# Rearranging what the graph stage issues around its matmuls: x loads, raw LSTM weight loads, staged sums, degree operations

## The chip, the cores and the metric

The kernel runs on one core of a Trainium2 chip. The metric is device time of one execution in microseconds (us), as the median of several executions. All data is float32.

## The reference

Four layers are applied to x of shape (128, 64, 256), each as x + layer(relu(layernorm(x))). Only the first one is touched by the change:

```python
h = relu(einsum('ts,bsh->bth', adj, x @ Wg0 + bg0))      # graph convolution 1
h = relu(einsum('ts,bsh->bth', adj, h @ Wg1 + bg1))      # graph convolution 2
for p in range(1, 5):                                    # windows of p tokens
    nw   = 64 // p
    wins = h[:, :nw * p].reshape(128 * nw, p, 256)
    last = lstm_last(Wih[p-1], Whh[p-1], bih[p-1], bhh[p-1], wins)
    h    = h.at[:, arange(nw) * p + (p - 1)].set(last)   # last state of each window
# layer 1: normalised adjacency (A + I scaled by 1/sqrt(degree)) and two batch norms
# layer 2: three products with diagonal, upper and lower part of adj;  layer 3: causal attention
```

The degrees of layer 1, deg = row sums + column sums - diagonal of A + I, are worked out early, beside the graph convolutions, because the engines have room there.

## The kernel before

**Two stages matter here.** The graph stage computes both graph convolutions for all tokens and leaves relu(h) transposed in the tiles hT. The LSTM stage then runs the four LSTMs out of hT. The tokens are cut into 16 slabs (NS = 16) of 512 tokens, four chunks of 128 each. One slab passes through three rounds of the graph stage: layernorm, aggregation with adj and the product with Wg0 in the first, aggregation again in the second, the product with Wg1 in the third. Three slabs are in flight at any time.

**The Strassen-like product.** The product with Wg1 uses seven half-size products instead of eight (`product`, L493). It needs four differences of the activations, which GpSimd makes (`sums`, L485), and matching sums of weights, which are made once (`weight_sum`, L313). The LSTM products do the same, in a form with more sums for p = 2, 3 and 4. Those weight sums are made on GpSimd during the graph stage and kept in DRAM until their LSTM runs. This is the staging:

- For each p of 2, 3, 4 the raw weights come in three groups of DMAs, issued by the SP queue (L363): W1 and W2 (the two halves of Whh, four DMAs of 128 KB each) and R (Wih, eight DMAs). They go to one working buffer, `wbf`, which all three p share, so each group can only be loaded when the sums before have been stored out of that part.
- 28 pieces of GpSimd work follow, each one instruction: additions 256 wide (L313), 512 wide (L370) and 384 wide (L377).
- Seven stores go back to DRAM, on the SP queue (L373, L394). The stores W1 (after piece 17), S4 (after piece 25) and S3 (after piece 27) are those that the next p's loads of W1, W2 and R must wait for.

The LSTM for p = 1 needs no such staging, only the tile `wih` (four loads at L308) and four sums of its own, 512 wide.

**The order is written by hand.** Every step is put into a list `events` with a time in planned microseconds, called order units below. The list is sorted by these times and the instructions are issued in that order. The times are not due times: each engine has its own queue, runs its instructions in the order of the list, and runs ahead as far as its waits allow. A round is `ROUND` = 10 units; slab s starts at 10 s. A staging piece n sits in slot n, six slots to a round:

```python
r, k = divmod(n, 6)
events.append((30 + ROUND * r + (-0.7, 0.5, 1.7, 2.9, 4.1, 5.3)[k], len(events), fn, ()))
```

In units modulo a round, GpSimd's order is: six pieces (-0.7 to 5.3), the four `sums` (7.2 to 8.05), the `root` of a layernorm (8.1, L439). "Round 90" below means the pieces that are placed from 89.3 on and the block of `sums` and root after them.

**VectorE's order** mixes the steps of three slabs: `stats` of the layernorm (L433, L434), then the input of the root (L438), `weighed` (L470, reads PSUM), the second step of the layernorm `shift` (L442, which waits for GpSimd's root and sits 3.0 units after it), and `begun` and `add` (L500, L507), which take the Strassen products out of PSUM. ScalarE copies the aggregated tiles out of PSUM (`aggregated`, L458), and applies the ReLUs (L446, L475, L523). PSUM has eight banks, taken in turn, so TensorE can start a product only when the add that reads the bank's former content has run.

**x loads.** `load` (L424) fetches one slab of 512 KB into one of three `xt` buffers. It is placed 21 units ahead of the slab, while the slab's `stats` start 15.1 units ahead.

**Degrees.** `adjacencies` is a generator with four steps, each run by `next` in one round: lbias, the sums of rows, the diagonal, and a last step with four VectorE instructions (L179 to L182). Then `degrees_root` (GpSimd, L185), `degrees` (VectorE, L189) and `normalize` (two matmuls at L209 and one VectorE instruction, L210).

Of the kernel before, what the change touches and what calls it, by code (L numbers as in the profile page):

```python
# [20 lines left out]
def kernel(ctx: ExitStack, tc: tile.TileContext, a: dict, out: bass.AP):  # L21
# [11 lines left out]
    NS = NT // SUP  # L33
# [132 lines left out]
    def adjacencies():  # L166

        nc.vector.tensor_add(lbias, con["bih"], con["bhh"])
        yield


        scr = first.tile([P, P], F32, tag="scr", name="scr")
        nc.vector.tensor_add(scr, adj_bd, ident)
        nc.vector.reduce_sum(deg[:, 0:1], scr, axis=AX.X)
        yield
        nc.vector.tensor_mul(scr, scr, ident)
        nc.vector.reduce_sum(deg[:, 1:2], scr, axis=AX.X)
        yield
        nc.vector.tensor_add(ahT, adjT_bd, ident)  # L179
        nc.vector.reduce_sum(deg[:, 2:3], ahT, axis=AX.X)  # L180
        nc.vector.tensor_add(deg[:, 0:1], deg[:, 0:1], deg[:, 2:3])
        nc.vector.tensor_sub(deg[:, 0:1], deg[:, 0:1], deg[:, 1:2])  # L182

# [3 lines left out]
    def degrees():  # L187
        dd = first.tile([P, P], F32, tag="dd", name="dd")
        nc.vector.tensor_scalar_mul(dd, ident, deg[:, 3:4])  # L189

        return dd
# [15 lines left out]
    def normalize(dd):  # L207
        ps = bank()
        nc.tensor.matmul(ps[:, :P], ones, dd, start=True, stop=True)  # L209
        nc.vector.scalar_tensor_tensor(ahT, ahT, deg[:, 3:4], ps[:, :P], op0=ALU.mult, op1=ALU.mult)  # L210
# [92 lines left out]
    def load_lstm(src, tag, pool):  # L303
        w = pool.tile([P, 7, 4, P], F32, tag=tag, name=tag)
        v = src.rearrange("(c p) (g h m) -> h c p g m", p=P, g=4, m=P)
        for h in range(2):
            for c in range(2):
                nc.sync.dma_start(w[:, 2 * h + c], v[h, c])  # L308
        return w

    def weight_sum(w, k):
        op = nc.gpsimd.tensor_sub if k else nc.gpsimd.tensor_add
        op(*(w[:, m] for m in ((S1, A21, A22), (S2, S1, A11), (S3, A11, A21), (S4, A12, S2))[k]))  # L313
# [96 lines left out]
    ROUND, HALF = 10.0, SUP // 2  # L410
    with tc.tile_pool(name="pa", bufs=2) as pa, tc.tile_pool(name="pax", bufs=3) as pax:
        events, wih0, made = [], [], []

        def graph_part(s):
            t0, v = ROUND * s, {}

            def at(t, fn, *args):
                events.append((t0 + t, len(events), fn, args))
# [104 lines left out]
                nc.scalar.activation(graphs(s, o), v["h2"][:, o, :].rearrange("p (q d t) -> p q d t", d=2, t=T),  # L523
                                     AF.Relu)

            at(-21, load)
            if s == 0:
                at(-20.5, first_constants)
                at(-10.5, second_constants)
# [16 lines left out]
            late, end = 0, s == NS - 1  # L546
# [8 lines left out]
            for c in range(KC):  # L555
                t = (0.86, 2.6)[c] if end else 4.35 + 0.89 * c
# [17 lines left out]
            at(late + 4.0, add, 0, 1, "b")  # L574
            at(late + 4.4, add, 1, 1, "a")
            at(late + 5.0, relu2, 0)
            at(late + 6.6, begun, 1, 0, "a")
            at(late + 7.1, relu2, 1)

            if s == 0:  # L580
# [5 lines left out]
                at(-9.5, lambda: weight_sums(con["wg1"]))  # L586
            if s == 4:
                pieces = adjacencies()
                for k in range(4):
                    at(5.0 + ROUND * k, next, pieces, None)  # L590
                at(11.5 + ROUND * 3, degrees_root)
                at(13.3 + ROUND * 3, lambda: made.append(degrees()))
            if s == 5:
                at(0, lambda: wih0.append(load_lstm(a["WihT"][0], "wih", lwa)))
            if s == 9:
                at(5.0, lambda: normalize(made[0]))
            if s == 9:
                for k in range(4):
                    at(1.4 + 1.3 * k, lambda k=k: weight_sum(wih0[0], k))

        for s in range(NS):
            graph_part(s)

        def stage(n, fn):
            r, k = divmod(n, 6)
            events.append((30 + ROUND * r + (-0.7, 0.5, 1.7, 2.9, 4.1, 5.3)[k], len(events), fn, ()))

        for i, p in enumerate(range(2, NL + 1)):
            work, stores, loads = staging(p)
            for n, fn in enumerate(work):  # L610
                stage(28 * i + n, fn)
            for n, fn in stores.items():
                stage(28 * i + n + 1, fn)
            for n, fn, t in zip((18, 26, 28), loads, (10.5, 17.5, 24.5)):
                if i:
                    stage(28 * (i - 1) + n + 1, fn)
                else:
                    events.append((t, len(events), fn, ()))
        for _, _, fn, args in sorted(events, key=lambda e: e[:2]):
            fn(*args)  # L620
    graph_weights.close()
# [105 lines left out]
    events = []  # L727

    def at(t, fn, *args):
        events.append((t, len(events), fn, args))  # L730
# [154 lines left out]
    def first_step(t0, st, tags, names):  # L885

        p, N = st["p"], st["N"]
        input_ = input_sums(st, 0)
        for k in (-9, -8.5, 0.2, 0.4) if st["new"] else (*((-0.8, -0.6) if p == NL else (-3.4, -1.4)), 2.6, 6.6):
            at(t0 + k, next, input_)  # L890
        g, end, t = {}, {}, t0
        for (name, gi, fn), tag in zip((g for g in GATES if g[0] != "f"), tags):
            g[name], end[name] = gate(t, st, p - 1, gi, fn, tag, names)
            t += 7
        e = end["g"]
        cell = cells[st["s"]]

        def start(n):
            i, g_ = (gates[g[k]["tag"]][:, n, :, :N] for k in "ig")
            nc.gpsimd.tensor_mul(cell[:, n, :, :N], i, g_)  # L900

        def squash(n):
            nc.scalar.activation(gates[g["g"]["tag"]][:, n, :, :N], cell[:, n, :, :N], AF.Tanh)

        h_at = t + 13.3
        for n in range(2):
            at(e + 2.2 + 0.1 * n, start, n)
            at(e + (6.07, 9)[n], squash, n)
            at(h_at + 0.8 * n, state, st, n, g["o"], g["g"], p == 1)
        st["h_at"] = h_at + 0.8  # L910
        return t
# [202 lines left out]
    t, tags = 0.0, [0, 1, 2, 3, 4]  # L1114
    plan(t, 2, (2, load_r), *((8 + 3 * k, fetch, name) for k, name in enumerate(("X", "W1", "W2", "S1", "S2"))),
         (25, fetch, "S4", 2, 7), (28, fetch_s3, 0))
    for p in range(1, NL + 1):
        pairs = pairs_of(p)
        for k in range(0, len(pairs), 2):
# [3 lines left out]
            for i, st in enumerate(sts):  # L1123
                if p == 1:
                    t = first_step(t, st, [tags[(3 * (k + i) + n) % 5] for n in range(3)], FIRST_BANKS)
                else:
# [4 lines left out]
                    t = first_step(t, st, tags[:3] if i == 0 else [*tags[3:], tags[0]], GROUP_BANKS)  # L1131
# [9 lines left out]
            for j in range(1, p):  # L1141
                for st in sts:
                    fin = p == NL and j == p - 1 and st is sts[-1]
                    u = t
                    t = outer_step(t, st, j, now, fin)
# [104 lines left out]
    with tc.tile_pool(name="pz", bufs=1, reuse_waits="tile") as pz:  # L1250
# [14 lines left out]
        events = []  # L1265
# [220 lines left out]
        late = ctx.enter_context(tc.tile_pool(name="late", bufs=1, side="right", reuse_waits="tile"))  # L1486
# [55 lines left out]
    with tc.tile_pool(name="pc", bufs=2, reuse_waits="tile") as pc, \  # L1542
            tc.tile_pool(name="pc1", bufs=1, reuse_waits="tile") as pc1:
        events = []
# [403 lines left out]
```

## Time and profile before

| what | us |
|---|---|
| median of 3 runs | 1836.33 (1835.55 to 1836.90) |
| the profiled execution, own time | 1838.82 |
| its span | 1837.10 |
| TensorE busy in the span | 1802.4 |
| graph stage, from the start to the first LSTM matmul | 178.70 |

The span is what the profile shows of the execution, from its first to its last instruction; the execution's own time also holds what lies around that (1.72 us here). The profiled execution is 2.49 us above the median of the runs. PE is TensorE's matmuls, PEld its weight loads, DVE VectorE, ACT ScalarE, POOL GpSimd and SP the queue that issues nearly all DMAs. In the timelines a line gives start, duration, engine, line of the kernel, operation, output and inputs, the number of like instructions that are merged, and in brackets how long the engine had been idle and what ended that. The granted TensorE clock was 1.00 in every stretch of the graph stage that is shown.

### The profile page before, as it was taken

Reading aid. Unit: us, or ns where it says so; the run is one execution under the profiler, and the core shown is the slowest. Engines: PE = TensorE matmul, PEld = TensorE weight load, DVE = VectorE, ACT = ScalarE, POOL = GpSimd, SP = SyncE. Lnnn points to the kernel's source line nnn. Section 1 sums busy time; section 2 is a strip of 40 time slices with the busy share of each in tenths; the row PEclk is TensorE's granted clock in tenths of the full one; section 3 lists DMA queues with packets and bytes.
Section 4 is the critical chain, followed back from the end, with each engine's and each line's share of the span. In section 5 each row is a group of like instructions: output and inputs, shape, how many; then the busy total and the mean of one; then the engine's idle time right before and its main releaser. Section 6 shows DMA issues by size and latency. Waiting matters only on the chain.

```text
span 1837.1 us, 24418 instructions
## 1 busy us (share of the span) xinstructions
PE 1802.4 (98%) x8532; PEld 1299.3 (71%) x8532; DVE 1196.0 (65%) x2346; ACT 990.8 (54%) x1776; POOL 1211.8 (66%) x1207
## 2 busy tenths in 40 slices
PE   8999999999999999999999999899999999999998
PEld 7987444466566887787466666566444899999997
DVE  6775555565666666666566666778776566666664
ACT  6765666644545545544644444678684444444442
POOL 5898455765766777776677776767354666666663
PEclk9999999999999999999999999999999999999999
DMA  5754300000003000003000000333200110111111
GB/s 149 242 181 174 115 1 0 6 1 9 6 23 115 1 1 1 1 1 113 26 0 1 1 1 30 109 115 115 70 3 1 47 33 26 47 47 47 47 47 35
DMA packets 67498, 91.20 MB, mean 50 GB/s; under 512 B 4784, under 2 KB 57776, under 8 KB 67376
## 3 DMA queue, kind: packets, MB, share of 16 engines
q1 hardware_dynamic: 66928, 89.35, 14.7%
q8 instruction: 68, 1.11, 0.3%
q14 instruction: 54, 0.44, 0.1%
q10 hardware_dynamic: 448, 0.30, 0.1%
HBM read 56.08 MB, written 33.55 MB: 49 GB/s over the span
## 4 chain that ended last, share of the span: by engine, by line
PE 89%; POOL 5%; ACT 2%; issue 2%; DVE 1%; DMA 1%; SPq 0%; POOLq 0%; DVEq 0%; ACTq 0%
PE ps L961 20%; PE ps L985 16%; PE ps L853 14%; PE ps L1672 8%; PE ps L1282 5%; PE ps L1399 4%; PE ps L1759 3%; PE ps L1639 3%; PE ps L454 2%; PE ps L1735 2%; PE ps L464 2%; PE ps L493 2%; PE ps L1769 2%; PE ps L1800 1%; PE ps L700 1%
## 5 line engine op out<-in xcount | busy, mean ns | idle before, releaser
L972 DVE TENSOR_TENSOR gate<-gate,ps 128x512 f32<-128x512 f32 (+2 forms) x360 | 216.7, 603 | 171.9 <-PE ps L961 160.1
L1005 ACT ACTIVATE gate<-gate,lbias 128x512 f32<-128x512 f32 (+2 forms) x288 | 175.7, 653 | 166.9 <-DVE gate L972 84.2
L866 DVE TENSOR_TENSOR gate<-gate,ps 128x512 f32<-128x512 f32 (+2 forms) x162 | 100.7, 640 | 128.7 <-PE ps L853 118.7
L970 ACT COPY gate<-ps 128x512 f32<-128x512 f32 (+2 forms) x144 | 74.9, 520 | 158.8 <-PE ps L961 158.3
L853 PE MATMUL ps<-tx,wih 128*128 128x512 f32 (+2 forms) x276 | 117.9, 544 | 3.0 <-ACT gate L869 2.5
L1615 ACT ACTIVATE h<-x,ln_rn 128x256 f32<-128x256 f32 x128 | 68.0, 592 | 92.8 <-POOL ln_rn L1612 92.7
L1015 POOL TENSOR_TENSOR gate<-gate 128x1024 f32<-128x1024 f32 (+3 forms) x37 | 73.5, 1986 | 63.1 <-ACT gate L1005 63.1
L862 ACT ACTIVATE gate<-gate,lbias 128x512 f32<-128x512 f32 (+2 forms) x108 | 95.7, 886 | 29.0 <-DVE gate L866 28.9
L1672 PE MATMUL ps<-wl,ag 128*128 128x128 f32 x900 | 108.4, 276 | 0.6
L1672 PEld LDWEIGHTS ps<-wl,ag 128*128 128x128 f32 x900 | 104.2, 192 | 3.3 <-ACT ag L1644 2.5
L961 PEld LDWEIGHTS ps<-h,wb 128*128 128x128 f32 x392 | 70.9, 190 | 41.2 <-issue 21.5
L999 DVE TENSOR_TENSOR gate<-gate,ps 128x512 f32<-128x512 f32 (+2 forms) x144 | 80.7, 602 | 21.6 <-PE ps L985 19.6
L961 PE MATMUL ps<-h,wb 128*128 128x256 f32 (+2 forms) x392 | 91.5, 356 | 1.9 <-POOL wb L947 1.3
L853 PEld LDWEIGHTS ps<-tx,wih 128*128 128x128 f32 x276 | 51.5, 190 | 57.1 <-issue 39.7
L818 POOL TENSOR_TENSOR tx<-hT 128x512 f32<-128x512 f32 (+2 forms) x29 | 36.0, 1242 | 79.2 <-PE ps L853 72.6
L869 ACT COPY gate<-ps 128x512 f32<-128x512 f32 (+2 forms) x108 | 59.4, 550 | 52.4 <-PE ps L853 51.8
L1018 POOL TENSOR_TENSOR cell<-cell,gate 128x1024 f32<-128x1024 f32 (+2 forms) x36 | 73.1, 2030 | 19.9 <-ACT gate L1005 19.9
L985 PE MATMUL ps<-hT,wb 128*128 128x512 f32 x160 | 81.7, 592 | 0.0
L900 POOL TENSOR_TENSOR cell<-gate 128x1024 f32<-128x1024 f32 (+2 forms) x36 | 78.1, 2191 | 5.4 <-ACT gate L862 5.4
L985 PE MATMUL ps<-wih,thA 128*128 128x512 f32 (+2 forms) x192 | 79.3, 495 | 0.0
L853 PE MATMUL ps<-hT,wih 128*128 128x512 f32 (+2 forms) x168 | 78.4, 571 | 0.0
L1021 POOL TENSOR_TENSOR cell<-cell,gate 128x1024 f32<-128x1024 f32 (+3 forms) x37 | 75.5, 2041 | 2.9
(333 smaller groups left out, 4981.5 us busy)
## 6 DMA issues: line engine op xcount, KB each, us to landing
xt<-in_x_dram SPq DMA_DIRECT2D x30, 512.0 KB, 4.4
x1d<-xt SPq DMA_DIRECT2D x16, 512.0 KB, 2.9
x<-x1d SPq DMA_DIRECT2D x16, 512.0 KB, 5.0
out_dram<-x SPq DMA_DIRECT2D x15, 512.0 KB, 3.4
W<-wb SPq DMA_DIRECT2D x6, 896.0 KB, 4.1
wb<-W SPq DMA_DIRECT2D x6, 896.0 KB, 4.9
wb<-in_WihT_dram SPq DMA_DIRECT2D x32, 128.0 KB, 3.4
wb<-in_WhhT_dram SPq DMA_DIRECT2D x24, 128.0 KB, 2.8
```

The lines of the kernel that those rows point to most:

```text
L853: nc.tensor.matmul(wide(p_[:, :N]), wih_of(p, k, gi), x_, start=first_, stop=True, skip_group_check=True)
L862: nc.scalar.activation(to, r[bank_][:, :N] if bank_ else to, fn, bias=lbias[:, l, m : m + 1])
L866: nc.vector.tensor_add(slot(n, hc), slot(n, hc), r[bank_][:, :N])
L900: nc.gpsimd.tensor_mul(cell[:, n, :, :N], i, g_)
L961: nc.tensor.matmul(B[pr, name][:, g * H : (g + 1) * H], w[:, g, :], d, start=(new and g == 0), stop=(name, k) in (("a", 4), ("b", 3), ("c" ...
L972: nc.vector.tensor_add(to, to, v)
L985: nc.tensor.matmul(to, w, d, start=(pr == 1 and c == 0), stop=(c == 1), skip_group_check=True)
L999: nc.vector.tensor_add(part(m, k), part(m, k), v)
L1005: nc.scalar.activation(v, v, FN[r, g], bias=lbias[:, l, b : b + 1])
L1021: nc.gpsimd.tensor_add(cell(n)[:, c], cell(n)[:, c], gate_(("11", "12")[n], 0)[:, c])
L1282: nc.tensor.matmul(r[name], con["w1"][:, OF[j], g, :], x_, start=new, stop=(name, j) in (("a", 4), ("b", 3), ("c", 2)), skip_group_check=True)
L1672: nc.tensor.matmul(v["g", name][:, p_, :], x_[:, m, ts(p_, P)], wl2[:, OF[j], m, :], start=new and p_ == m == 0, stop=m == 2 and (name, j) ...
```

## The change

No instruction that computes is added or removed, and no DMA either. What changes is the place of instructions in the list, and so their order on each engine:

- The x loads of slabs 3 to 15 are placed 26 units ahead of the slab instead of 21.
- The staging starts at slot 3 of a list of slots that begins at 20 instead of 30: three slots into a round one earlier, 6.4 units ahead. After the 28 pieces of p = 2 come the four `wih` sums as pieces of their own (before, they stood at 91.4 to 95.3, besides the six pieces of that round). After the 28 of p = 3 two slots stay empty. The last piece so moves from 165.3 to 171.7.
- The raw loads of a next p no longer stand in the slot after the store that they wait for, but at the end (9.01) of the round in which that slot lies. For p = 3 they stand at 59.01, 69.02 and 79.03 (before: 60.5, 72.9, 75.3), for p = 4 at 109.01, 129.02 and 129.03 (before: 105.3, 120.5, 122.9). Slab 10's x load, for example, moves from behind the R loads of p = 3 to ahead of them. For p = 2 the three are at 9.01, 11 and 19.01 instead of 10.5, 17.5 and 24.5.
- The last step of `adjacencies` is cut in two, so that it takes five rounds. `degrees_root`, `degrees` and `normalize` follow one round later.
- For slab 14 the last `begun` stands at 6.15 instead of 6.6, which puts it ahead of the direct product of slab 15 on VectorE.

```diff
@@ adjacencies
         nc.vector.tensor_add(ahT, adjT_bd, ident)
         nc.vector.reduce_sum(deg[:, 2:3], ahT, axis=AX.X)
+        yield
         nc.vector.tensor_add(deg[:, 0:1], deg[:, 0:1], deg[:, 2:3])
         nc.vector.tensor_sub(deg[:, 0:1], deg[:, 0:1], deg[:, 1:2])
@@ graph_part
-            at(-21, load)
+            at(-21 if s < 3 else -26, load)
...
-            at(late + 6.6, begun, 1, 0, "a")
+            at(late + (6.15 if s == NS - 2 else 6.6), begun, 1, 0, "a")
...
             if s == 4:
                 pieces = adjacencies()
-                for k in range(4):
+                for k in range(5):
                     at(5.0 + ROUND * k, next, pieces, None)
-                at(11.5 + ROUND * 3, degrees_root)
-                at(13.3 + ROUND * 3, lambda: made.append(degrees()))
+                at(11.5 + ROUND * 4, degrees_root)
+                at(13.3 + ROUND * 4, lambda: made.append(degrees()))
             if s == 5:
                 at(0, lambda: wih0.append(load_lstm(a["WihT"][0], "wih", lwa)))
-            if s == 9:
+            if s == 10:
                 at(5.0, lambda: normalize(made[0]))
-            if s == 9:
-                for k in range(4):
-                    at(1.4 + 1.3 * k, lambda k=k: weight_sum(wih0[0], k))
@@ after the slabs
+        START = (9.01, 11, 19.01)
+        PHASE = (-0.7, 0.5, 1.7, 2.9, 4.1, 5.3)
+
         def stage(n, fn):
             r, k = divmod(n, 6)
-            events.append((30 + ROUND * r + (-0.7, 0.5, 1.7, 2.9, 4.1, 5.3)[k], len(events), fn, ()))
-
+            events.append((20 + ROUND * r + PHASE[k], len(events), fn, ()))
+
+        at_piece = 3
         for i, p in enumerate(range(2, NL + 1)):
             work, stores, loads = staging(p)
             for n, fn in enumerate(work):
-                stage(28 * i + n, fn)
+                stage(at_piece + n, fn)
             for n, fn in stores.items():
-                stage(28 * i + n + 1, fn)
-            for n, fn, t in zip((18, 26, 28), loads, (10.5, 17.5, 24.5)):
-                if i:
-                    stage(28 * (i - 1) + n + 1, fn)
-                else:
-                    events.append((t, len(events), fn, ()))
+                stage(at_piece + n + 1, fn)
+            for fn, t in zip(loads, START if i == 0 else after):
+                events.append((t, len(events), fn, ()))
+            full = [at_piece + n for n in (17, 25, 27)]
+            after = [20 + ROUND * ((n + 1 - (n + 1) % 6) // 6) + 9.01 + 0.01 * k for k, n in enumerate(full)]
+            at_piece += 28
+            if i == 0:
+                for k in range(4):
+                    stage(at_piece + k, lambda k=k: weight_sum(wih0[0], k))
+                at_piece += 4
+            else:
+                at_piece += 2
```

## The prediction

> **What bounds the kernel now.** First the page: which engine fills the span, and where the fill is missing.
>
> ```profile
> PE 1802.4 (98%) x8532; PEld 1299.3 (71%) x8532; DVE 1196.0 (65%) x2346; ACT 990.8 (54%) x1776; POOL 1211.8 (66%) x1207
> ...
> PE   8999999999999999999999999899999999999998
> ...
> POOL 5898455765766777776677776767354666666663
> ```
>
> TensorE is busy for 98%, so only its holes can be won. The edit touches the graph stage, the first 182 us (slices 1 to 4). There the list of waits gives TensorE three: "PE ps L493 <- DVE h L507", 2.3 us once, and "<- DVE h L500", 2.8 us twice. I cut the stage from one start of the L464 matmuls (one a round) to the next:
>
> ```profile
> 79.55:89.44 9.89, 9.89 (x64) 9.12 (x63) 7.21 (x20) 7.19 (x13) 6.60 (x10) 1.00 0.77 217
> 89.44:102.25 12.81, 10.51 (x65) 9.41 (x64) 8.46 (x24) 7.57 (x13) 12.20 (x13) 1.00 0.38 142
> 102.25:114.78 12.53, 10.60 (x63) 9.19 (x62) 7.53 (x19) 7.21 (x13) 12.37 (x15) 1.00 0.49 167
> 114.78:124.90 10.12, 10.12 (x63) 9.24 (x62) 7.33 (x18) 7.32 (x13) 9.89 (x13) 1.00 0.73 248
> 124.90:134.95 10.05, 10.05 (x63) 9.28 (x62) 7.38 (x21) 7.38 (x13) 8.56 (x11) 1.00 0.56 188
> 134.95:146.23 11.28, 10.34 (x64) 9.27 (x63) 7.17 (x19) 7.30 (x13) 8.78 (x11) 1.00 0.75 218
> ```
>
> Columns: stretch, length, then busy us of PE, PEld, DVE, ACT, POOL. An undisturbed round takes 10.05 us and is all TensorE; three take 12.81, 12.53 and 11.28. Why, the timelines of DVE, POOL and the DMA queue SP say:
>
> ```profile
> 92.03 0.43 DVE L433 BATCH_NORM_STATS2 ln_st<-xt 128x6 f32<-128x256 f32 x1 [4.19 <-DMA xt<-in_x_dram]
> 110.45 0.68 DVE L442 SCALAR_TENSOR_TENSOR ln_rn<-ln_mv,ln_rn 128x4 f32<-128x4 f32 x1 [2.94 <-POOL ln_rn L439]
> 141.89 0.68 DVE L442 SCALAR_TENSOR_TENSOR ln_rn<-ln_mv,ln_rn 128x4 f32<-128x4 f32 x1 [1.68 <-POOL ln_rn L439]
> ...
> 89.86 2.54 POOL L370 TENSOR_TENSOR wc<-wb 128x512 f32<-128x512 f32 x2 [2.79 <-DMA wb<-in_WihT_dram]
> 98.84 1.27 POOL L313 TENSOR_TENSOR wih<-wih 128x512 f32<-128x512 f32 x1
> 137.29 0.73 POOL L313 TENSOR_TENSOR wb<-wb 128x256 f32<-128x256 f32 x1 [3.47 <-issue]
> ...
> 81.93 5.92 SPq L363 DMA_DIRECT2D wb<-in_WihT_dram  x8
> 87.96 0.96 SPq L424 DMA_DIRECT2D xt<-in_x_dram  x2
> 132.94 1.91 SPq L363 DMA_DIRECT2D wb<-in_WhhT_dram  x4
> ```
>
> **Hole 1** (2.30 us at 97.55): the x load of slab 10 stood behind eight raw-weight DMAs (87.96), VectorE waited 4.19 us for it, and the h2 adds that free PSUM banks stood behind that. **Hole 2** (1.86 us at 111.57): GpSimd had four `wih` sums of 1.24 us besides its six pieces between 96.36 and 106.54; its root came 2.94 us late to VectorE's shift. **Hole 3** (0.94 us at 143.02): GpSimd waited 3.47 us for a raw load which the SP queue could issue only at 132.94, because the S4 store, issued at 125.10, took 7.82 us to land.
>
> **What the Trainium skill says.** "PSUM — Partial Sum Buffer", section "Engine vs sequencer instructions": ScalarE, VectorE and GpSimdE queues are strict FIFO. The trace agrees: at 110.45 VectorE held back ready adds. "DMA: Bandwidth & Descriptors", section "Anatomy of one DMA — SWDGE (gpsimd) path": DMA engines do not wait on semaphores; the issuing sequencer does, before dispatch. Agrees: raw loads (L363) held SP for 12.1 us in four waits on stores. "SBUF — State Buffer", section "Who interferes with whom": a VectorE tensor_tensor with both inputs in SBUF contends with GpSimd's reads. Agrees as far as it goes: the 128x128 add at L179 took 0.72 us, the same form at L173 0.26.
>
> **The ceiling.** Round starts run 29.06, 39.11, 49.16, 59.29, 69.34, 79.39, 89.44, 102.25, 114.78, 124.90, 134.95, 146.23, 156.56, 166.61. From 29.06 to 166.61 are 137.55 us for 13 rounds; 13 x 10.05 = 130.65. Excess 6.90, of which 0.22 is the two matmuls of `normalize`, which only change rounds. So **6.68 us** can come back: the three holes (5.10) and slowed products beside them (two of four at 107.46 wait for `t`, 0.33; first products after a hole and the round after each, 1.25 together).
>
> **Part by part.**
>
> *x loads of slabs 3 to 15, five units earlier in the order.* No DMA is added. On SP, slab 10's load now stands before the eight R loads of p=3 instead of behind. Ahead of it is the S3 store, which waits for GpSimd's last piece of p=2. I place that piece at 74.75: root 8 ends at 73.49, piece 27 takes 1.25. So the load goes out near 75.4, and by the page's median of 4.4 us it lands near 80; VectorE wants it near 87.9. 8 us spare, hole 1 goes. Its xt buffer (three of them) was freed by ReLUs of slab 7, eleven order units earlier, so SP does not stop there. Each earlier load adds 0.4 us of SP time ahead of raw loads. That costs nothing while they have the spare time given below. Slab 3's load now precedes the `parts_d` store, which held SP 4.5 us until 15.07.
>
> *`wih` sums as four pieces between p=2 and p=3, and the staging one round earlier.* GpSimd's work per round is 3.9 us of `sums` and root plus pieces. In an undisturbed round the root ends at 83.64 and the second sum can start at 90.5 (80.45 + 10.05, ScalarE's copy), less 0.7 for the first sum: room for 6.1 us of pieces. With 0.70 us for 256 wide, 1.0 for 384, 1.25 for 512, rounds of pieces before, from 30 on: 4.2, 6.4, 5.3, 5.4, 5.3, 5.85, **10.2**, 5.9, 4.8, 5.3, 6.4, 4.7, 5.9, 5.3. Trace for the bold one: 10.18. After, from 20 on: 2.1, 5.9, 4.75, 6.15, 5.05, **6.9**, 4.75, 6.4, 5.6, 5.1, 3.9, 4.75, 5.85, 5.6, 5.1, tail 3.2. Worst is 6.9, 0.8 over the room. The root has slack: normally it ends 0.96 us before the shift (83.64 to 84.60), and a shift late by 2.94 and 1.68 cost 1.86 and 0.94, so another 0.74 to 1.08 is absorbed. Together 1.7 to 2.0 us; 0.8 fits and the next round (4.75) pays it back. Hole 2 goes. If the cover were gone, 0.8 us.
>
> *Raw loads at fixed places after their stores.* p=3: R's use comes after five 256-wide pieces, at 83.64 + 3.5 = 87.1. W2 needs the S4 store (67.2, lands near 71.2), R's last four the S3 store (74.75, near 78.5); eight issues end by 81, landing 83.5. Spare 3.6 us; the 2.79 wait goes. p=4: S4 is done at 124.5, S3 at 127.0. The S4 store lands after 3.8 us (median of these stores) or 7.8 (longest), W2's loads are out by 130.2 or 134.2 and land by 133 or 137; wanted at 135.2. R, right behind, lands by 136 or 140; wanted at 137.3 at the earliest. GpSimd's wait is 0 to 2.7 us in a round with 1.3 us room and 1.7 slack: TensorE loses **0**. Behind these loads no x load is queued any more. Hole 3 goes. I take 0 and keep 1 us for the range.
>
> *Two empty slots before p=4; later end.* GpSimd's last piece ends at 171.2 by this count (before: 175.1), though later in the order. Its next work, `tx` (L818), waited 6.63 us for hT; with the stage 6.7 us shorter that leaves 2.8. Nothing.
>
> *Degree operations.* The same DVE instructions (0.72 + 0.29, then 0.38 + 0.16) now in two rounds, root (0.55 POOL) and `normalize` a round later; ahT is used only after the LSTM stage. Nothing in a DVE with over 2 us idle a round; with that cover gone 0.5.
>
> *`begun` of slab 14 ahead of the direct product.* 0.47 us of DVE moves from 179.57 to before 178.91. ScalarE's ReLUs run in the old order and start at 179.69 on the direct product, so nothing; bounds -0.4 to +0.3.
>
> *Earlier GpSimd pieces in round 20*: they fill a 4.63 us idle stretch before 28.59. If they slow DVE's small operations, 0 to 0.3.
>
> **Sum.** -6.68, plus 0.3 for DVE contention and rounds that do not close fully: -6.4. Against the profiled execution's own 1838.82 (span 1837.10): 1832.4. That execution lies 2.5 above the median of the runs, so against 1836.33: **1829.9**. What follows is TensorE work in the LSTM stage and shifts as a whole.
>
> **Rivals.** *One hole stays or a new one opens* (R2), for instance in round 70, or after late p=4 loads: 1.5 to 4 us, giving 1831.5 to 1834. For it: POOL is booked with 5.85 us or more in five rounds of 6.1. *No gain* (R3): SP stops before the x loads, since all stores in front of them wait for GpSimd; holes 1 and 3 return elsewhere, 1834 to 1837. Against it: every x load has 8 us or more. *Slower* (R4): the p=4 raw loads, bound to 129 in the order, land so late that GpSimd stands in the middle of round 130 with `sums` 12 behind. TensorE loses the wait less 3.0 us (1.3 + 1.7). It eats the gain from a wait of 9.7 us on, and makes the kernel 0.2% slower from 13.4 on, that is W2 landing at 148.6: some 1840.5. Against it: with the longest store seen W2 lands at 137. That the change does not do what it says is part of R3: order is not time, and SP runs ahead wherever it may.
>
> **Numbers.** A measurement of this kernel can tell about 0.2% (3.7 us) from no change. All holes closed: 0.76, 1829 to 1831. R2 0.13, half of it beyond 1832.7. R3 0.05, R4 0.06. Faster by over 0.2%: 0.76 + 0.06 = 0.82, less 0.03 for holes of which I see only the first layer: 0.79. Within: 0.14. Slower: 0.07. The range reaches from 1828.9 (the end effect of 0.4 and a little below) to 1833.0, into R2.
>
> **What would show it.** Right: round starts 10.0 to 10.1 us apart from 29 to about 160, one 0.22 longer; no L433 wait on xt near 88; no L442 wait over 2 us on L439; `wih` sums near 75; hT's last ReLU some 6.5 us earlier. Wrong: a round over 11 us, a GpSimd wait over 4 us on a raw load, or a first LSTM matmul (178.70 before) later than 175 us.

## The result, and the profile after

| | before, us | after, us |
|---|---|---|
| median of 15 runs each, first comparison | 1837.56 | 1833.29 |
| ratio, first comparison | | 0.9974 [0.9966, 0.9981] |
| ratio, second comparison (`after_again`) | | 0.9977 [0.9967, 0.9987] |
| profiled executions, own time | 1838.82, 1838.52, 1837.41 | 1832.69, 1832.86 |

Faster by 0.26% (4.8 us by the first ratio), where 0.35% (6.4 us) was forecast; 6.4 us lies just outside the first interval, whose faster end is 6.2 us. The first comparison's median includes three disturbed executions (2697, 4866 and 6743 us), which its ratio leaves out, and the profiled execution that came with it, one of them, ran at a granted clock of 0.655, so the trace after is that of `after_again`, the same kernel run again.

The stretches from one round start to the next, in `after_again` (columns as in the prediction: stretch, length, busy us of PE, PEld, DVE, ACT, POOL, then clock and DMA):

```profile
79.01:89.06 10.05, 10.05 (x64) 9.28 (x63) 7.80 (x19) 7.28 (x13) 9.74 (x14) 1.00 0.69 205
89.06:99.11 10.05, 10.05 (x64) 9.28 (x63) 8.89 (x23) 7.35 (x13) 9.49 (x12) 1.00 0.07 26
99.11:109.38 10.27, 10.27 (x66) 9.50 (x65) 7.88 (x22) 7.57 (x13) 8.11 (x10) 1.00 0.83 273
109.38:119.87 10.49, 10.33 (x63) 9.26 (x62) 7.48 (x19) 7.21 (x13) 10.25 (x14) 1.00 0.58 209
119.87:129.92 10.05, 10.05 (x63) 9.27 (x62) 7.45 (x19) 7.38 (x13) 8.44 (x11) 1.00 0.68 230
129.92:139.97 10.05, 10.05 (x64) 9.28 (x62) 7.47 (x19) 7.27 (x13) 8.69 (x12) 1.00 0.82 218
```

The rounds of 12.81, 12.53 and 11.28 us are gone. One round is 0.22 longer for the two matmuls of `normalize`, one 0.44 for a new small loss. The timelines of the same run show what answers to the three waits. VectorE:

```profile
104.28 0.75 DVE L443 SCALAR_TENSOR_TENSOR ln_rn<-ln_mv,ln_rn 128x4 f32<-128x4 f32 x1
```

GpSimd:

```profile
74.31 5.15 POOL L314 TENSOR_TENSOR wih<-wih 128x512 f32<-128x512 f32 x4
87.75 1.30 POOL L371 TENSOR_TENSOR wc<-wb 128x512 f32<-128x512 f32 x1
107.10 2.50 POOL L371 TENSOR_TENSOR wb<-wb 128x512 f32<-128x512 f32 x2 [2.09 <-DMA W<-wb]
138.09 1.31 POOL L371 TENSOR_TENSOR wc<-wb 128x512 f32<-128x512 f32 x1 [0.21 <-issue]
```

The queue SP:

```profile
67.06 0.34 SPq L374 DMA_DIRECT2D S<-wb  x1
76.53 0.38 SPq L425 DMA_DIRECT2D xt<-in_x_dram  x1
76.97 5.46 SPq L364 DMA_DIRECT2D wb<-in_WihT_dram  x8
128.64 2.64 SPq L364 DMA_DIRECT2D wb<-in_WhhT_dram  x4
```

(After the change lines 180 and later stand one line further down, so L443 is the shift.) The shift that had waited 2.94 us no longer waits; the `wih` sums run near 75; the first use of p=3's R at 87.75 does not wait, that of p=4 waits 0.21 us. What is new is the 2.09 us wait of GpSimd at 107.10 for a store. It makes the next root late: the next slab's shift waits 0.62 us for it at 115.26, and TensorE then stands for a moment:

```profile
116.66 0.70 PE L494 MATMUL ps<-g,wg 128*128 128x256 f32 x2 [0.16 <-DVE h L501]
```

The end of the stage, on TensorE:

```profile
172.88 1.98 PE L861 MATMUL ps<-hT,wih 128*128 128x512 f32 x4 [0.55 <-DVE h L501]
174.70 1.02 PE L861 MATMUL ps<-ready,wih 128*128 128x512 f32 x2
175.94 1.13 PE L861 MATMUL ps<-ready,wih 128*128 128x512 f32 x2 [0.22 <-ACT gate L877]
176.91 1.88 PE L861 MATMUL ps<-hT,wih 128*128 128x512 f32 x4
```

In the kernel before, the group that corresponds to the last of these lines was

```profile
183.07 1.88 PE L853 MATMUL ps<-hT,wih 128*128 128x512 f32 x4
```

I use this fourth group of LSTM matmuls as the mark for the end of the stage. It starts at 176.91 (before: 183.07), 16.85 us after the last round start; before it was 16.46.

### The profile page after: what moved, and what is told of

It reads as the page before. It is cut to its first block, busy times and chain, and to the rows that moved or that the text cites. A ratio compares the mean times of both kernels' runs of the same rounds, so it can differ in the third digit from the quotient of the medians.

```text
span 2695.0 us, 24421 instructions
## 1 busy us (share of the span) xinstructions
PE 2680.4 (99%) x8532; PEld 1605.8 (60%) x8532; DVE 1198.1 (44%) x2346; ACT 1006.6 (37%) x1776; POOL 1178.5 (44%) x1207
## 4 chain that ended last, share of the span: by engine, by line
PE 99%; DVE 0%; ACT 0%; DMA 0%; issue 0%; DVEq 0%
PE ps L969 21%; PE ps L993 18%; PE ps L861 17%; PE ps L1680 8%; PE ps L1290 5%; PE ps L1407 5%; PE ps L455 3%; PE ps L465 3%; PE ps L1767 3%; PE ps L1743 3%; PE ps L494 3%; PE ps L1647 2%; PE ps L1777 2%; PE ps L708 2%; PE ps L1808 2%; PE ps L666 1%
## 5 line engine op out<-in xcount | busy, mean ns | idle before, releaser
L861 PE MATMUL ps<-tx,wih 128*128 128x512 f32 (+2 forms) x276 | 172.6, 760 | 0.0
L1680 PE MATMUL ps<-wl,ag 128*128 128x128 f32 x900 | 155.8, 348 | 0.0
L1680 PEld LDWEIGHTS ps<-wl,ag 128*128 128x128 f32 x900 | 150.3, 256 | 4.6 <-ACT ag L1652 2.6
L969 PE MATMUL ps<-h,wb 128*128 128x256 f32 (+2 forms) x392 | 131.9, 475 | 0.7 <-ACT h L670 0.7
L969 PEld LDWEIGHTS ps<-h,wb 128*128 128x128 f32 x392 | 82.1, 211 | 84.4 <-issue 52.3
L993 PE MATMUL ps<-hT,wb 128*128 128x512 f32 x160 | 119.5, 839 | 0.0
L861 PE MATMUL ps<-hT,wih 128*128 128x512 f32 (+2 forms) x168 | 115.4, 806 | 0.0
L993 PE MATMUL ps<-wih,thA 128*128 128x512 f32 (+2 forms) x192 | 114.4, 688 | 0.0
L861 PE MATMUL ps<-tx,wb 128*128 128x512 f32 x144 | 101.4, 838 | 0.0
L969 PEld LDWEIGHTS ps<-tx,wb 128*128 128x128 f32 x288 | 60.8, 215 | 58.5 <-issue 39.0
```

The lines of the kernel that those rows point to most:

```text
L861: nc.tensor.matmul(wide(p_[:, :N]), wih_of(p, k, gi), x_, start=first_, stop=True, skip_group_check=True)
L969: nc.tensor.matmul(B[pr, name][:, g * H : (g + 1) * H], w[:, g, :], d, start=(new and g == 0), stop=(name, k) in (("a", 4), ("b", 3), ("c" ...
L993: nc.tensor.matmul(to, w, d, start=(pr == 1 and c == 0), stop=(c == 1), skip_group_check=True)
L1680: nc.tensor.matmul(v["g", name][:, p_, :], x_[:, m, ts(p_, P)], wl2[:, OF[j], m, :], start=new and p_ == m == 0, stop=m == 2 and (name, j) ...
```

## The experiments

All trace numbers are of one profiled execution each. "13 rounds" is from the third round start (near 29) to the last (near 160 or 166), 137.55 us in the execution on which the prediction was made.

### The changed kernel again, and parts of it

> The changed kernel once more, for its trace at full TensorE clock. My theory (all three holes of 6.68 us in the round starts close): round starts 10.05 us apart from 29 to about 160, total 137.55 - 6.7 = 130.9 for the 13 rounds, ratio 0.9965. The rival, that a hole of 1 to 2 us stays in round 70 or after the late raw loads of p=4: one or two rounds of 11 us or more, 132 to 133 in all, ratio 0.9973.

Measured: 13 rounds in 131.29 us, no round over 10.49. The holes are shut; the ratio, 0.9977, is nearer the rival's.

**x loads alone** (on the kernel before):

```diff
-            at(-21, load)
+            at(-21 if s < 3 else -26, load)
```

> The kernel before with the x loads of slabs 3 to 15 five units earlier and nothing else. If the holes are independent, hole 1 closes and 2.8 us come back (ratio 0.9985). My theory now: between 90.4 and 110 us GpSimd is the chain (its sums at 92.4, root at 95.3, six pieces and four wih sums to 106.5), and an earlier x does not move it; hole 1 shrinks to about 1 us, hole 2 grows by what hole 1 lost, and nothing or under 0.7 us comes back (ratio 0.9996 to 1.0).

Measured: 136.90 us, ratio 1.0003 [0.9994, 1.0011]: nothing. The two rounds together take 26.20 us, and took 25.34. VectorE no longer waits for x near 88, but GpSimd's root comes late, since the first use of R waits longer than before (3.81 us, against 2.79, 3.12 and 1.83 in three traces of the kernel before: the x load now runs ahead of R). The timeline of VectorE in `x_only`:

```profile
97.66 1.22 DVE L442 SCALAR_TENSOR_TENSOR ln_rn<-ln_mv,ln_rn 128x4 f32<-128x4 f32 x1 [2.62 <-POOL ln_rn L439]
111.64 0.68 DVE L442 SCALAR_TENSOR_TENSOR ln_rn<-ln_mv,ln_rn 128x4 f32<-128x4 f32 x1 [3.62 <-POOL ln_rn L439]
```

Of GpSimd and of TensorE:

```profile
91.23 2.56 POOL L370 TENSOR_TENSOR wc<-wb 128x512 f32<-128x512 f32 x2 [3.81 <-DMA wb<-in_WihT_dram]
```

```profile
99.33 0.70 PE L493 MATMUL ps<-g,wg 128*128 128x256 f32 x2 [2.40 <-DVE h L500]
112.77 0.70 PE L493 MATMUL ps<-g,wg 128*128 128x256 f32 x2 [1.86 <-DVE h L500]
```

Hole 1 has another releaser and the same size. GpSimd was the second layer behind the x load; I had not followed it when I gave hole 1 to the x load. My new theory underrated it too (1 us expected, 2.40 measured).

**Staging, raw loads and `wih` sums alone** (the change with the x loads, the degrees and the last `begun` as before):

> The changed kernel with the x loads back at 21 units ahead, and the degrees and the last begun of slab 14 as before: only the staging, the wih sums and the raw loads stand in their new places. In this list slab 10's x load stands at 79.00, just ahead of the R loads of p=3 at 79.03, so theory A says hole 1 closes without the earlier x loads and the whole gain is here: 13 rounds in 130.7 to 131.2 us, ratio as after_again within 0.0003. Rival B, that the x loads need the five units more: a DVE wait of 2 us or more on an x load and 1 to 3 us less gained.

Measured: 130.91 us, no wait on x, ratio 0.9970 [0.9959, 0.9982]. Theory A holds: the whole gain is here. The fourth LSTM group starts 16.46 us after the last round start, as in the kernel before. (Slab 10's x load still goes out just ahead of the R loads here, at 75.57; `raw_slots` below takes that away.)

**Degrees and the last `begun` alone:**

> The kernel before with only the degree operations spread over five rounds and the last begun of slab 14 moved ahead. Theory: no change, 13 rounds in 137.3 to 137.8 us, ratio 0.9997 to 1.0003. Rival: the VectorE block of 1.55 us at 78.3 delays something that hole 1 hides, then up to 0.5 us comes back.

Measured: 136.90 us, ratio 1.0010 [1.0002, 1.0018]. Against my expectation the time is slightly over the kernel before's. The trace shows one new wait: `degrees` on VectorE waits 1.91 us for GpSimd's `degrees_root`, which now stands in the crowded round 90 behind the `wih` sums. TensorE does not stop for it: from 98.36 to 111 it works without a hole, though at half its clock from 99.01 to 102.42 (the clock is taken up in the last section). The 13 rounds lie within those of three traces of the kernel before. The record of the single executions says more: 6 of the 13 of `rest_only` have a mean granted clock of 0.997, against 4 of the 57 of the kernel before, while at 0.999 and 0.998 the two kernels' means lie within 0.5 us of each other. So much of the 0.1% goes with a lower clock; why this kernel has it more often stays open. The stage's end takes 16.45 us.

### The kernel before twice more, the crowded round, the raw loads' places

> The kernel before, unchanged, for a second trace. Theory: hole 3 (1.5 us with the round after it) was the luck of one execution, in which the S4 store of p=3 took 7.82 us; two relatives with the same raw loads had no hole there. Then this trace shows rounds of 10.0 to 10.3 us after 125 and 13 rounds in 136.2 to 137.0 us. Rival: hole 3 belongs to the kernel, a round over 10.8 us between 125 and 160.

> The kernel before, unchanged, for a third trace. As the second: no round over 10.8 us after 125 by the theory that hole 3 is an accident of one store's landing; one such round by the rival. Holes 1 and 2 (rounds of 12 to 14 us between 89 and 116) in both theories.

Measured: 137.67 and 136.16 us. Neither has a round over 10.14 us after 117: hole 3 is the accident of one execution, in which the S4 store took 7.8 us to land (6.2 and 5.8 in these). But my total for `before_b`, at most 137.0, was wrong: these two have something else. One round takes 14.7 us in each, and its mean granted clock is 0.88. Stretches of `before_b`:

```profile
89.12:101.58 12.46, 10.52 (x66) 9.42 (x65) 8.88 (x24) 7.56 (x13) 11.61 (x12) 1.00 0.32 117
101.58:116.26 14.68, 12.49 (x63) 10.86 (x62) 7.36 (x19) 8.12 (x14) 14.45 (x18) 0.88 0.55 194
```

Of `before_c`:

```profile
89.39:104.06 14.67, 12.17 (x66) 10.82 (x65) 8.01 (x24) 7.66 (x13) 13.38 (x15) 0.88 0.43 147
104.06:114.91 10.85, 10.33 (x63) 9.26 (x62) 7.19 (x19) 7.20 (x13) 10.69 (x14) 1.00 0.42 148
```

Just after a hole TensorE runs slowly for some 3.4 us; in `before_b`, on its timeline:

```profile
111.42 0.70 PE L493 MATMUL ps<-g,wg 128*128 128x256 f32 x2 [1.86 <-DVE h L500]
111.96 0.62 PE L493 MATMUL ps<-t,wg 128*128 128x256 f32 x2
112.41 3.45 PE L454 MATMUL ps<-adjT_bd,h 128*128 128x128 f32 x16
```

Sixteen such matmuls take 1.95 us elsewhere. The drop costs 1.5 us here, and 0.17 on the next group (0.77 instead of 0.60).

**The `wih` sums back in round 90** (on the changed kernel):

```diff
-                    stage(at_piece + k, lambda k=k: weight_sum(wih0[0], k))
+                    events.append((91.4 + 1.3 * k, len(events), lambda k=k: weight_sum(wih0[0], k), ()))
```

> The changed kernel with the four wih sums back at 91.4 to 95.3, besides six pieces; their slots in the staging stay empty. Theory: GpSimd's round 90 grows from 6.4 to 11.4 us, root 11 ends near 108.6 instead of 103.6, VectorE's shift (wanted near 104.3) comes 4.3 us late, 0.74 to 1.08 of it is absorbed: a hole of 3.2 to 3.6 us and up to 0.5 us beside it; the 2.09 us wait for the W2 store near 107 goes. 13 rounds in 134.2 to 135.0 us, ratio to the kernel before near 0.9990. Rival: the staging's earlier start alone made the room, and the loss is under 1.5 us.

Measured: 134.44 us, 3.15 more than the changed kernel, inside the range; the median is 1836.87 us, 3.9 over the changed kernel's 1832.98 of the second comparison, and the ratio 0.9999 [0.9990, 1.0008] holds the expected 0.9990 only at its edge. The wait for the W2 store is gone, as said. The loss sits in two places, though, not in one (the timelines of VectorE and of TensorE):

```profile
97.47 1.29 DVE L190 TENSOR_SCALAR dd<-ident,deg 128x128 f32<-128x128 f32 x1 [1.66 <-POOL deg L186]
108.41 0.68 DVE L443 SCALAR_TENSOR_TENSOR ln_rn<-ln_mv,ln_rn 128x4 f32<-128x4 f32 x1 [3.09 <-POOL ln_rn L440]
```

```profile
99.56 0.67 PE L494 MATMUL ps<-t,wg 128*128 128x256 f32 x2 [0.73 <-DVE h L508]
109.54 0.70 PE L494 MATMUL ps<-g,wg 128*128 128x256 f32 x2 [1.86 <-DVE h L501]
```

The degree root stands in the crowded round as in `rest_only` and holds VectorE; the shift then waits 3.09 us and TensorE stands 1.86 us. So the spread of the `wih` sums is worth some 3 us in the trace. The staging's earlier start without it would be worth 2.7 us by traces (134.44 against a mean of 137.13 before), but the ratio allows 1.8 us at most. The profiled execution is one of the quicker ones: six executions with a mean granted clock of 0.999, it among them, took 1835.2 to 1836.8 us, the six with a lower clock 1836.9 to 1839.8.

**The raw loads in the slot after their stores** (on the changed kernel):

```diff
-            full = [at_piece + n for n in (17, 25, 27)]
-            after = [20 + ROUND * ((n + 1 - (n + 1) % 6) // 6) + 9.01 + 0.01 * k for k, n in enumerate(full)]
+            after = [20 + ROUND * ((at_piece + n) // 6) + PHASE[(at_piece + n) % 6] for n in (19, 27, 29)]
```

> The changed kernel with the raw loads of p=3 and p=4 in the slot after the store that they wait for, as in the kernel before; slab 10's x load is then behind p=3's R loads again. Theory: since the whole staging stands 6.4 units earlier, R is out by 83 us and the x load lands by 88, when VectorE wants it; no hole, 13 rounds within 0.5 us of the changed kernel's 131.3. Rival: the order on SP is what made hole 1, then VectorE waits 2 us or more on xt near 88 and a round takes over 11 us.

Measured: 131.54 us. Slab 10's x load goes out at 81.93 behind R's eight, and no DVE wait follows. p=4's R makes GpSimd wait 2.26 us, within the bound of 2.7, and one round takes 10.23: two tenths. The queue SP in `raw_slots`, then the S4 store of p=2 in the kernel before:

```profile
81.93 0.95 SPq L425 DMA_DIRECT2D xt<-in_x_dram  x2
```

```profile
74.91 0.34 SPq L373 DMA_DIRECT2D S<-wb  x1
```

The fixed places bring next to nothing; what shut hole 1 is the earlier start, by which that store goes out at 67.06 (67.08 in `raw_slots`) instead of 74.91.

### The two small losses

**x loads back at 21 units** (on the changed kernel):

> The changed kernel with the x loads of all slabs back at 21 units ahead. Theory: hole 1 stays shut, since the staging's earlier start did that; and slab 12's x load goes out behind the W2 store of p=3 instead of just ahead of it, so that store lands within 6.5 us (8.5 in the changed kernel), GpSimd does not wait 2.1 us for it at 107, and the round of 10.49 us becomes 10.05: 13 rounds in 130.8 to 130.95 us. Rival: the 8.5 us are chance, the wait stays or comes and goes with no tie to the x load, 131.2 to 131.6; or the earlier x loads are needed and a round takes over 11 us.

Measured: 130.86 us; no wait for the W2 store, which landed in 6.1 us. Stretches:

```profile
99.64:109.91 10.27, 10.27 (x65) 9.50 (x64) 7.39 (x22) 7.50 (x13) 10.11 (x13) 1.00 0.76 268
109.91:119.96 10.05, 10.05 (x63) 9.27 (x62) 7.43 (x19) 7.19 (x13) 9.10 (x12) 1.00 0.86 260
```

The queue SP in `after_again` and then in `x_back`:

```profile
98.07 0.39 SPq L425 DMA_DIRECT2D xt<-in_x_dram  x1
98.55 0.86 SPq L374 DMA_DIRECT2D W<-wb  x1
```

```profile
98.87 0.34 SPq L374 DMA_DIRECT2D W<-wb  x1
99.31 0.53 SPq L425 DMA_DIRECT2D xt<-in_x_dram  x1
```

Behind the x load the store took 8.5 us to land, in all four kernels with that order whose staging stands as in the change (`after_again`, `after_c`, `raw_slots`, `begun_back`); ahead of it at most 6.5 us, in all three (`staging_only`, `x_back`, `both_back`). In `wih_late`, where it was issued 1.5 us behind the x load instead of 0.5, it took 7.2 us. The x loads' move costs 0.4 to 0.5 us here and brings nothing.

**The last `begun` back at 6.6:**

> The changed kernel with the last begun of slab 14 at 6.6 again. Theory: the 0.55 us idle of TensorE before the first LSTM matmul goes (it waits for that begun, which now stands behind a subtraction that VectorE finishes late), and with the 0.66 us wait after it back in place of 0.22, the end of the graph stage takes 0.3 to 0.4 us less: 16.4 to 16.5 us from the last round start to the fourth group of LSTM matmuls, against 16.85 in the changed kernel and 16.46 before. Rival: the end is set by the late subtraction (1.55 us instead of 0.68) in either order, 16.8 us or more.

Measured: the opposite of the theory. The fourth LSTM group comes 17.13 us after the last round start. TensorE stands 1.28 us until 173.53, which is 0.1 us after the `begun` ended at 173.43:

```profile
173.53 1.96 PE L861 MATMUL ps<-hT,wih 128*128 128x512 f32 x4 [1.28 <-issue]
175.32 1.96 PE L861 MATMUL ps<-ready,wih 128*128 128x512 f32 x4
```

**Both back:**

> The changed kernel with both the x loads and the last begun back: of the change only the staging, its raw loads, the wih sums and the degree operations are left. If both small losses are real, 0.4 us in the rounds and 0.4 us at the end come back: 13 rounds in 130.9 us, fourth group of LSTM matmuls at 176.0 to 176.3 us after an equal start, ratio to the kernel before 0.0004 under the changed kernel's. By the rival (chance), the same as the changed kernel.

Measured: 130.85 us in the rounds, as expected; 17.13 at the end, as in `begun_back`; ratio 0.9974 [0.9963, 0.9984]. So the moved `begun` is worth 0.28 us (17.13 to 16.85), on top of a loss of 0.67 (16.46 to 17.13) that `staging_only` does not have; the degree operations are all that differs between it and `both_back`. They act through the PSUM banks, which are not taken strictly in turn. The bank numbers in the built programs show it: in all of them the first LSTM matmul writes bank 0, but what bank 0 held last is, in the kernel before and in `staging_only`, an aggregated tile that ScalarE copied out earlier, and, wherever `normalize` stands one round later, slab 14's product "a", which this `begun` reads last.

Placed at 6.6, the `begun` runs 12.96 us after the last round start before the change, in `staging_only` and in `both_back` (12.97 in `begun_back`). TensorE is ready for the LSTM at 12.1. Before the change and in `staging_only` its first LSTM matmul does not need the bank that the `begun` reads; in the other two it does, and has to wait. Placed at 6.15 in `rest_only`, the `begun` is early enough (177.66, 11.42 us after the round start), and nothing is lost: 16.45. In the changed kernel it comes only at 12.30, behind a subtraction on VectorE that takes 1.55 us, on the timeline of `after_again`:

```profile
170.88 1.55 DVE L406 TENSOR_TENSOR ready<-hT,ready 128x512 f32<-128x512 f32 x1
172.36 0.47 DVE L501 SCALAR_TENSOR_TENSOR h<-rs_row,bg,ps 128x256 f32<-128x256 f32 x1
```

The subtraction is slow beside the last two GpSimd pieces, which the later end of the staging has moved there. That alone costs nothing: `staging_only` has it too, and there TensorE starts before the `begun` (GpSimd, VectorE and TensorE):

```profile
169.00 2.95 POOL L370 TENSOR_TENSOR wb<-wb 128x512 f32<-128x512 f32 x2
170.94 1.55 DVE L405 TENSOR_TENSOR ready<-hT,ready 128x512 f32<-128x512 f32 x1
173.09 0.47 DVE L500 SCALAR_TENSOR_TENSOR h<-rs_row,bg,ps 128x256 f32<-128x256 f32 x1
172.23 1.88 PE L860 MATMUL ps<-hT,wih 128*128 128x512 f32 x4
```

So the moved `begun` makes good what the moved degree operations cost, and the later end of the staging takes more than half of that back.

**The changed kernel a third time:**

> The changed kernel a further time, for a second undisturbed trace. Theory: the 2.1 us wait for the W2 store near 107 and the round of 10.4 to 10.6 us are there again, and the 0.55 us before the first LSTM matmul; 13 rounds in 131.1 to 131.6 us. Rival, that they are chance: no such wait, 130.9 us.

Measured: 131.35 us, a round of 10.54, the wait of 2.1 us, 0.57 us before the first LSTM matmul. The small losses are no chance.

By traces `staging_only` is the best version: from the third round start to the fourth LSTM group it takes 147.37 us, the changed kernel 148.14 and 148.20. The intervals of the two ratios overlap, but at the same mean granted clock of 0.999 five of its six executions average 1832.14 us and the changed kernel's nine, in the same comparison, 1833.02: 0.9 us, where the traces say 0.8.

## Why the prediction was right or wrong

**The sum.** The direction was right, and the ceiling nearly so. In traces, the fourth LSTM group starts at 183.07, 182.97 and 181.71 (mean 182.58) before and at 176.91 and 177.13 (mean 177.02) after: 5.56 us. The profiled executions' own times differ by 5.5 us (means 1838.25 and 1832.78), the comparisons by 4.2 to 4.8. Of the 6.68 counted:

- *The ceiling, hole 3 in it*: the ceiling came from one execution. Its 13 rounds took 137.55 us; the mean of three is 137.13, 0.42 less. Hole 3 was in one of three, and the other two had a clock drop that I could not see in mine. I noted that the profiled execution lay 2.5 us above the median and then took its holes at full size.
- *"Each earlier load adds 0.4 us of SP time ahead of raw loads. That costs nothing"*: I looked at raw loads and not at stores. The x load ahead of p=3's W2 store cost 0.44 and 0.49 us in two traces.
- *"`begun` ... so nothing", "Degree operations ... Nothing", "later end ... Nothing"*: together 0.39 us (16.46 to 16.85). The term that failed is the degree operations': through the PSUM banks they cost 0.67 us. The moved `begun` makes up for all of it in `rest_only`, but for only 0.28 beside the later end of the staging. The last two GpSimd pieces, 2.97 us instead of 2.5, now overlap VectorE's subtraction of the LSTM's first inputs (1.55 us instead of 0.68), where before they had ended at 175.08 and it began at 177.42. Both operations read two inputs in SBUF, and both got longer, as the Trainium skill ("SBUF — State Buffer", section "Who interferes with whom") has it for this pair. I quoted that and applied it to small operations only. The sum for `tx` was also wrong: its own figures leave 3.8 us of the 6.63, not 2.8, and 3.66 were measured.
- The round starts begin 0.15 us earlier (29.00 to 28.85 in the means). I had not counted it, and it may be chance: over all thirteen traces they begin between 28.63 and 29.40.

6.68 - 0.42 - 0.47 - 0.39 + 0.15 = 5.55, the 5.56 of the traces. The difference between 5.5 and the 4.2 to 4.8 of the comparisons lies mostly with the kernel before: its three profiled executions average 1838.25, 0.6 to 1.0 above its medians in the four comparisons (1837.29 to 1837.65), while those of the changed kernel lie at theirs (1832.98). The first ratio's interval holds both. The absolute 1829.9 was also missed because the base was: 1836.33 on three runs became 1837.56 on fifteen.

**The steps.** *Hole 1 by the x loads*: wrong cause. `x_only` leaves it as large, and it stays shut with the x loads back at 21 units (`x_back`, `staging_only`) and with slab 10's load behind R again (`raw_slots`). It is shut by the staging's earlier start. That hole 1 closed as priced was luck: another part of the same change did it. *Hole 2 by the `wih` sums*: right; `wih_late` brings back 3.15 us. The count of pieces per round was good: root 11 was to wait for 6.4 us of pieces and degree root in round 90, and the trace has 93.31 to 99.73. In round 70, the 6.9 us over the room of 6.1 cost nothing: that round took 10.05 us. *Absorbed lateness of 0.74 to 1.08*: right at its lower end, and only up to some 2 us. A shift late by 1.26, 1.68 and 1.99 us (`before_c`, before, `rest_only`) made holes of 0.52, 0.94 and 1.25 us: 0.74 less each time (in the changed kernel a lateness of 0.62 still made 0.16, so the room is not the same in every round). A shift late by 2.94, 3.09, 3.46 and 3.62 us (before, `wih_late`, `before_b`, `x_only`) made a hole of 1.86 us every time, so the 1.08 came from a case where the hole no longer grows with the lateness. That TensorE was already held by GpSimd's `t` just before (0.22 and 0.39 us in two of these traces) would explain the fixed size, but was not tested. *p=4's raw loads*: right; GpSimd waited 0.21, in `raw_slots` 2.26, against 0 to 2.7 bounded, and TensorE lost 0 and 0.2. *R4* did not come near (1836.33 and 0.2% make 1840.0, not its 1840.5).

## What to carry to other kernels

When a wait is named in a trace, ask what would end next if it went: here an x load hid a GpSimd that was just as late, and moving the x load alone gave nothing. Before a hole is priced, look at it in a second execution; one of the three in this one was not there in the next two. When an in-order queue is rearranged, count what is moved ahead of stores as well as of loads, since a store that lands late holds whoever reuses its buffer. And when a change has several parts, look for one that only makes good what another costs: here the moved `begun` is of use only because the degree operations were moved.

## What the runs showed of the hardware

TensorE's clock drops to half for 3.41 us at a time, or twice that, in the records of single executions. The drops lie where TensorE has just stood idle. After the start (the first matmul comes near 6.6) and up to its end, a trace of these kernels has no TensorE idle of 1.8 us or more except the large holes of the graph stage, nine in six of the traces (1.86 to 2.50 us), and one wait of 3.1 us for ScalarE, which ends between 1185 and 1192 in all thirteen; from the waits of `after_again`:

```profile
PE ps L1290 <- ACT hS L1295: 3.1, 1, 3.1
```

All fourteen drops begin within 1.2 us of the end of one of these, before or after it. Three of the nine holes of 1.86 to 2.50 us have one (in `before_b`, `before_c` and `rest_only`), and eleven of the thirteen waits of 3.1 us; the two idles of 1.7 us that every trace has, near 585 and 1182, have none. The two executions without a drop at the 3.1 us wait (`staging_only`, `begun_back`) have the shortest remainders after the fourth LSTM group, 1652.4 us both; with one drop it is 1653.8 to 1654.1, with one of double length 1655.5 and 1655.3 (`x_only`, `both_back`). So a drop of 3.41 us costs 1.4 to 1.7 us. That the idle causes the drop is not tested, and it does not always follow.

In these traces a mean granted clock of 1.000 means no drop, 0.999 one, and 0.998 two or a double one. By that reading 35 of 57 recorded executions of the kernel before have two or more, and 3 of 21 undisturbed ones of the changed kernel. The ten of the kernel before at 1.000 took 1835.4 to 1836.9 us, the four at 0.997 took 1839.1 to 1840.5. This is a good part of the 5 us over which single runs of one kernel spread, and of why profiles told these versions apart better than times. If the idle is the cause, a long hole costs more than its length.
